# Graph attention in two layers: a closing product in seven half-size products, row maxima by way of DRAM, joins on VectorE, last residuals a unit ahead

## Chip, cores, metric

One core of a Trainium2 chip. The metric is the device time of one execution in microseconds (us), the median of several runs. "Before" took 1975.14 us (1974.1 to 1975.79) when the prediction was made.

## The reference

```python
def layer0(x, adj, weight):                    # N = 4096 rows, D = 512
    return relu(adj @ (max(sign(x), 0) @ sign(weight).T))
def layer1(x, adj, weight, bias, node_w, edge_w):
    node_att = softmax(x @ node_w, axis=0)
    h = x @ edge_w
    e = where(adj > 0, h @ h.T, NEG_BIG)
    return adj * (node_att * softmax(e, axis=1)) @ (x @ weight) + bias
x = layernorm(x + layer0(x, adj, ...))
x = layernorm(x + layer1(x, adj, ...))
```

Everything is float32. TensorE sets the time (it is busy for 1954.7 of 1974.9 us), so the kernel saves multiplications wherever it can: the large products use Strassen-like schemes with seven products for eight.

## The kernel before

It has four stretches. In the *first phase* (to about 500 us) layer 0 is summed up: `adj` is split in a rounded part `hi` and a rest `lo`, both stationary operands for the rows `xw`. Then come the scores `h @ h.T`, which go to DRAM (`s_d`) with their row maxima and sums. In the *main loop* (from 1079.6 us) four groups of four *blocks* reload scores, shift them by the row maximum, exponentiate, weigh by `adj` and multiply (tile `ps`). Each finished group is *joined* (seven additions) and gets its *closing product* with `w1`, whose instructions are put between those of the next group's blocks. The last group's closing product is the *tail*.

The row maxima `nm` stand one per partition. The shift needs them along the free dimension, the same line in all partitions. Before, TensorE did that:

```python
def panel(A):                                   # 512 rows: P = 128 partitions, BG = 4 row blocks
    nm = small.tile([P, BG], F32, name="nm")    # pool `small` has 2 buffers of each tile
    ...                                         # (cut: factor f of the softmax)
    spread = rows.tile([P, BG, P], F32, name="spread", tag="rows")
    nc.vector.tensor_copy(spread, nm.unsqueeze(2).to_broadcast([P, BG, P]))
    pt = ps_tr.tile([P, BG, P], F32, name="ptm", tag="tr")
    for i in range(BG):
        nc.tensor.transpose(pt[:, i, :], spread[:, i, :], ident)
    ...
    nc.scalar.copy(mrow.rearrange("p (b w) -> p b w", w=P), pt)

# the shift that uses the line, VectorE then ScalarE
    m = mrow.unsqueeze(1).to_broadcast([P, BG, W])
    pinned[0](nc.vector._custom_dve(TENSOR_ADD_SAT, out=q, in0=q, in1=m, s0=0.0, s1=-HUGE))
    nc.scalar.activation(q, q, AF.Exp)

# the closing product, one row block
    for k in range(KD):
        nc.tensor.matmul(po, (lower if k // 2 else upper)[:, k % 2, ts(i, P)], w1_s[:, k, :], ...)
    nc.vector.scalar_tensor_tensor(xb, po, f[:, i : i + 1], xb, ALU.mult, ALU.add)
```

## Time and profile before

| | before |
|---|---|
| time, median of 3 | 1975.14 us |
| TensorE busy | 1954.7 of 1974.9 us |
| first aggregation matmul starts at | 1079.6 us |
| main loop, first to last aggregation matmul | 854.3 us |
| tail | 41.0 us |

The last three are read from the start of the first and the end of the last `ps` matmul in the trace. Before the tail TensorE has no pause above 2.1 us. The page also has a picture of the span in 40 slices of 49 us; here are its rows for TensorE's busy tenths and the bytes moved by all DMA engines:

```profile
PE   9999999999999999999999999999999999999997
GB/s 312 297 322 304 305 320 315 296 327 279 154 266 201 189 284 255 225 258 287 198 365 310 351 270 236 269 253 196 217 264 253 212 252 236 225 288 206 160 60 64
```

### The profile page before, as it was taken

To read this page: it belongs to the slowest core of one execution; us is meant where nothing else is said; L and a number is where in the kernel's file an instruction comes from. 1 tells how busy PE (TensorE), PEld (TensorE's weight loads), DVE (VectorE), ACT (ScalarE), POOL (GpSimd) and SP (SyncE) were. 2 spreads that over 40 slices of the span, in tenths; PEclk is the share of its full clock that TensorE was granted. 3 is DMA by queue.
4 is the path that set the end of the run, shared out by engine and by line. 5 is a ranking of instruction groups with operands and counts; after the bars stand their busy time and mean duration, and the time that the engine had idled before them with its cause. 6 is when DMAs were issued, how large, how long until landed. Compare 5 with 4: busy or idle time off the path is not lost.

```text
span 1974.9 us, 18126 instructions
## 1 busy us (share of the span) xinstructions
PE 1954.7 (99%) x6122; PEld 1088.6 (55%) x6122; DVE 1365.8 (69%) x1992; ACT 672.7 (34%) x1107; POOL 402.4 (20%) x507
## 2 busy tenths in 40 slices
PE   9999999999999999999999999999999999999997
PEld 6888888888544455444555444444444444444443
DVE  7767667667764576667466986968678866967634
ACT  5433333333103576666677311121112211131100
POOL 0122222223341111101022111431124121411101
PEclk9999999999999999999999999999999999999999
DMA  8888888887475576677598976775677576675421
GB/s 312 297 322 304 305 320 315 296 327 279 154 266 201 189 284 255 225 258 287 198 365 310 351 270 236 269 253 196 217 264 253 212 252 236 225 288 206 160 60 64
DMA packets 133645, 497.71 MB, mean 252 GB/s; under 512 B 14000, under 2 KB 14000, under 8 KB 125872
## 3 DMA queue, kind: packets, MB, share of 16 engines
q0 software_dynamic: 71488, 262.17, 35.4%
q1 hardware_dynamic: 53712, 205.02, 31.0%
q10 hardware_dynamic: 8352, 29.36, 4.2%
q8 instruction: 48, 0.79, 0.2%
q14 instruction: 45, 0.37, 0.1%
HBM read 376.96 MB, written 119.54 MB: 251 GB/s over the span
## 4 chain that ended last, share of the span: by engine, by line
PE 91%; DMA 3%; issue 2%; DVE 2%; ACT 1%; POOL 1%; POOLq 0%; DVEq 0%; SPq 0%; ACTq 0%
PE ps L887 39%; PE seven L699 12%; PE acc L371 11%; PE acc L370 11%; PE po L940 5%; PE pe L630 4%; PE seven L98 4%; PE pt L600 2%; DMA s_d<-slot 2%; PE acc L243 1%; PE pw L211 1%; PE pt L330 1%; ACT line L571 1%; PE acc L244 1%; DMA more<-in_adj_dram 0%
## 5 line engine op out<-in xcount | busy, mean ns | idle before, releaser
L887 PE MATMUL ps<-lent,lop 128*128 128x512 f32 x960 | 419.3, 592 | 0.0
L370 PE MATMUL acc<-xw,hi 128*128 128x512 f32 x960 | 376.4, 392 | 0.0
L371 PE MATMUL acc<-xw,lo 128*128 128x512 f32 x960 | 374.3, 390 | 0.0
L887 PE MATMUL ps<-slot,lop 128*128 128x512 f32 x832 | 364.0, 592 | 0.0
L887 PEld LDWEIGHTS ps<-lent,lop 128*128 128x128 f32 x960 | 182.0, 190 | 227.2 <-issue 221.0
L887 PEld LDWEIGHTS ps<-slot,lop 128*128 128x128 f32 x832 | 157.8, 190 | 197.8 <-issue 193.2
L362 DVE TENSOR_TENSOR lo<-at,hi 128x1024 fp32r<-128x1024 f32 x120 | 147.0, 1225 | 84.4 <-ACT hi L360 84.3
L371 PEld LDWEIGHTS acc<-xw,lo 128*128 128x128 f32 x960 | 180.3, 188 | 37.1 <-DVE lo L362 0.3
L370 PEld LDWEIGHTS acc<-xw,hi 128*128 128x128 f32 x960 | 180.3, 188 | 36.8
L360 ACT CAST hi<-at 128x1024 fp32r<-128x1024 f32 x120 | 126.4, 1054 | 203.4 <-PE acc L370 148.4
L891 DVE TENSOR_TENSOR over<-over,ps 128x512 f32<-128x512 f32 x168 | 113.6, 680 | 94.0 <-PE ps L887 93.7
L804 ACT ACTIVATE lent<-lent 128x2048 f32<-128x2048 f32 x32 | 61.1, 1910 | 252.4 <-DVE lent L803 239.3
L630 PE MATMUL pe<-hT 128*128 128x512 f32 (+3 forms) x384 | 132.1, 486 | 0.0
L562 DVE CUSTOM_DVE_ANT_0 line<-lent,slot 128x512 f32<-128x512 bf16 x144 | 93.0, 688 | 45.9 <-ACT slot L640 23.0
L571 ACT ACTIVATE line<-line,nmax_c 128x512 f32<-128x512 f32 x160 | 114.8, 724 | 22.2 <-DVE nmax_c L562 22.1
L940 PE MATMUL po<-over 128*128 128x512 f32 x256 | 115.9, 600 | 3.2 <-DVE xb L949 3.2
L803 DVE CUSTOM_DVE_ANT_1 lent<-lent,line 128x2048 f32<-128x2048 f32 x32 | 80.9, 2527 | 49.6 <-DMA lent<-s_d 49.5
L804 ACT ACTIVATE slot<-slot 128x2048 f32<-128x2048 f32 x32 | 61.1, 1910 | 131.2 <-DVE slot L803 120.0
L699 PE MATMUL seven<-hT 128*128 128x512 f32 x192 | 89.8, 593 | 0.0
L630 PEld LDWEIGHTS pe<-hT 128*128 128x128 f32 x384 | 64.6, 191 | 41.4 <-issue 33.8
L940 PEld LDWEIGHTS po<-over 128*128 128x128 f32 x256 | 49.1, 192 | 65.9 <-issue 60.4
L803 DVE CUSTOM_DVE_ANT_1 slot<-slot,line 128x2048 f32<-128x2048 f32 x32 | 75.1, 2353 | 11.4 <-DMA slot<-s_d 10.2
(205 smaller groups left out, 2497.1 us busy)
## 6 DMA issues: line engine op xcount, KB each, us to landing
at<-in_adj_t_dram SPq DMA_DIRECT2D x60, 1024.0 KB, 7.2
lop<-lop_d SPq DMA_DIRECT2D x112, 512.0 KB, 3.9
lent<-in_adj_t_dram POOLq DMA_DIRECT2D x34, 1024.0 KB, 7.2
s_d<-slot POOLq DMA_DIRECT2D x33, 1024.0 KB, 7.0
slot<-s_d POOLq DMA_DIRECT2D x32, 1024.0 KB, 7.7
lent<-s_d POOLq DMA_DIRECT2D x32, 1024.0 KB, 8.3
slot<-in_adj_t_dram POOLq DMA_DIRECT2D x30, 1024.0 KB, 7.4
lent<-in_adj_dram SPq DMA_DIRECT2D x48, 512.0 KB, 5.0
```

The costliest lines, as they stand in the source:

```text
L360: nc.scalar.copy(hi, aq)
L362: nc.vector.tensor_sub(lo, aq, hi.bitcast(F32))
L370: nc.tensor.matmul(acc, hi[:, c, :], xw[:, kb, :], start=(kb == 0), stop=False)
L371: nc.tensor.matmul(acc, lo[:, c, :], xw[:, kb, :], start=False, stop=(kb == NB - 1))
L571: nc.scalar.activation(line, line, AF.Exp, bias=nmax_c[:, b, c : c + 1], scale=-1.0, accum_out=sum_c[:, b, c : c + 1])
L630: nc.tensor.matmul(pe[:, lo * P :], hT[:, k, ts(A * BG + i, P)], hT[:, k, (B * BG + lo) * P : (B + 1) * W], start=(k == 0), stop=(k == KD ...
L699: nc.tensor.matmul(ps, left[m][:, k, q, :], right[m][:, k, :], start=(first and k == 0), stop=(k == KD // 2 - 1), skip_group_check=not first,)
L803: pinned[0](nc.vector._custom_dve(TENSOR_ADD_SAT, out=q, in0=q, in1=m, s0=0.0, s1=-HUGE))
L804: nc.scalar.activation(q, q, AF.Exp)
L887: nc.tensor.matmul(ps, lop[:, c, ts(h, P)], rop[:, c, :], start=(c == 0), stop=(c == BG - 1))
L891: nc.vector.tensor_add(total[:, m, h, :], total[:, m, h, :], ps)
L940: nc.tensor.matmul(po, (lower if k // 2 else upper)[:, k % 2, ts(i, P)], w1_s[:, k, :], start=(k == 0), stop=(k == KD - 1),)
```

## The change

Four parts: eight quarter products of the closing product become seven of half width; the row maxima are written to DRAM and read back as a line into all partitions; the joins go from GpSimd to VectorE; the last group's residuals are loaded one block earlier. The steps put between the blocks also come twice as often, most of the normalizing moves to ScalarE, and the last outputs leave by SyncE's queue instead of GpSimd's. The core of the diff (the new class for the closing product is cut):

```diff
+    nm_d = [dram.tile([W], F32, name=f"nm_d{g}") for g in range(NG)]
@@ panel
-        spread = rows.tile([P, BG, P], F32, name="spread", tag="rows")
-        nc.vector.tensor_copy(spread, nm.unsqueeze(2).to_broadcast([P, BG, P]))
-        pt = ps_tr.tile([P, BG, P], F32, name="ptm", tag="tr")
-        for i in range(BG):
-            nc.tensor.transpose(pt[:, i, :], spread[:, i, :], ident)
         mrow = take(free_e)
-        nc.scalar.copy(mrow.rearrange("p (b w) -> p b w", w=P), pt)
+        nc.scalar.dma_start(nm_d[A].rearrange("(b p) -> p b", p=P), nm)
+        nc.gpsimd.dma_start(mrow, nm_d[A].unsqueeze(0).to_broadcast([P, W]))
@@ closing product (cut)
+            nc.vector.tensor_add(s1, l21, l22)          # and three more combinations
+            yield lambda: multiply("y", l11, 0, (a, 0))  # and six more half-width products
@@ normalizing, all but the last group
+                less = small.tile([P, n], F32, name="less")
+                nc.vector.scalar_tensor_tensor(less, mv[:, :, 0], -1.0, rstd, ALU.mult, ALU.mult)
+                nc.scalar.activation(xb, xb, AF.Identity, bias=less[:, k : k + 1], scale=rstd[:, k : k + 1])
@@ main loop
-            for queue, share in ((first, ...), (todo, count[0] % 2)):
+            for queue, share in ((first, ...), (todo, 1)):
-            todo.extend(lambda g=u.g, n=n: join(g, n, nc.gpsimd) for n in range(7))
+            todo.extend(lambda g=u.g, n=n: join(g, n, nc.vector) for n in range(7))
+        if n == len(blocks) - 2:
+            todo.extend(e.load for e in ends_)
```

More of the change, by code (lines that the diff above doesn't have):

```diff
@@ L772, in panel @@
         mrow = take(free_e)
-        nc.scalar.copy(mrow.rearrange("p (b w) -> p b w", w=P), pt)
+        nc.scalar.dma_start(nm_d[A].rearrange("(b p) -> p b", p=P), nm)
+        nc.gpsimd.dma_start(mrow, nm_d[A].unsqueeze(0).to_broadcast([P, W]))
         panels[A] = f, mrow
+        made[A] = now[0]
+    made = {}
     pinned = [tc.keep_in_program_order]
@@ L870, in landed, with known @@
                 return lambda: self.since[n] + 5 <= now[0]
+            def known(n):
+                return lambda: max(self.since[n], made[self.g + n % 2 * HG]) + 5 <= now[0]
             for k, n in enumerate(order):
-                yield landed(n), lambda n=n: self.shift(n)
+                yield known(n), lambda n=n: self.shift(n)
                 yield landed(4 + n), lambda k=k, n=n: self.weigh(n, order[k + 2] if k < 2 else None)
@@ L913, in join, with __init__ @@
         engine.tensor_tensor(out_, a, b, op)
+    spare = []
     class Finish:
-        def __init__(self, g, half, single=False):
-            self.g, self.half, self.A, self.single = g, half, g + half * HG, single
+        def __init__(self, g, half, last=False):
+            self.g, self.half, self.A, self.last = g, half, g + half * HG, last
+            self.stats = {}
         def steps(self):
             yield self.load
-            for i in range(BG):
-                yield lambda i=i: self.row(i)
-            if not self.single:
-                yield lambda: self.norm(range(BG))
+            for q in range(2):
+                yield from self.pair(q, ps_tr)
+            yield lambda: self.norm(range(BG))
         def load(self):
+            rows_ = x1_d[self.A * W : (self.A + 1) * W, :]
+            if self.last:
+                xb = take()
+                nc.gpsimd.dma_start(xb, rows_.rearrange("(b p) d -> p b d", p=P))
+                self.xbs = [xb[:, i, :] for i in range(BG)]
+                return
             self.xbs = []
@@ L931, in load @@
                 xb = rows.tile([P, D], F32, name="xb1", tag="rows")
-                nc.gpsimd.dma_start(xb, x1_d[ts(self.A * BG + i, P), :])
+                nc.gpsimd.dma_start(xb, rows_[ts(i, P), :])
                 self.xbs.append(xb)
-        def row(self, i):
-            t = sums[:, self.g % 2]
-            upper, lower = (t[:, 2], t[:, 4]) if self.half else (t[:, 1], t[:, 3])
-            po = ps_tr.tile([P, D], F32, name="po", tag="tr")
-            for k in range(KD):
-                nc.tensor.matmul(
-                    po,
-                    (lower if k // 2 else upper)[:, k % 2, ts(i, P)],
-                    w1_s[:, k, :],
-                    start=(k == 0),
-                    stop=(k == KD - 1),
-                )
-            f, _ = panels[self.A]
-            xb = self.xbs[i]
-            nc.vector.scalar_tensor_tensor(xb, po, f[:, i : i + 1], xb, ALU.mult, ALU.add)
-            if self.single:
-                self.norm([i])
@@ L953, in norm, with pair, combine, multiply @@
-        def norm(self, some_):
-            layernorm([self.xbs[i] for i in some_])
-            for i in some_:
-                nc.gpsimd.dma_start(out[ts(self.A * BG + i, P), :], self.xbs[i])
+        def pair(self, q, pool):
+            sums_g = sums[:, self.g % 2]
+            upper, lower = (sums_g[:, 2], sums_g[:, 4]) if self.half else (sums_g[:, 1], sums_g[:, 3])
+            a, b = q, q + 2
+            l11, l12, l21, l22 = (x[:, :, ts(i, P)] for i in (a, b) for x in (upper, lower))
+            tag = "tr" if pool is ps_tr else "mm"
+            bank, s = {}, []
+            def combine():
+                s.append(lopp.tile([P, 4, KD // 2, P], F32, name="left1", tag="lop"))
+                s1, s2, s3, s4 = (s[0][:, n] for n in range(4))
+                nc.vector.tensor_add(s1, l21, l22)
+                nc.vector.tensor_sub(s2, s1, l11)
+                nc.vector.tensor_sub(s3, l11, l21)
+                nc.vector.tensor_sub(s4, l12, s2)
+            def multiply(name, lop, rop, *to):
+                first = name not in bank
+                if first:
+                    x = name == "x"
+                    bank[name] = (ps_mm if x else pool).tile([P, HD], F32, name="po", tag="mm" if x else tag)
+                po = bank[name]
+                lop = lop if not isinstance(lop, int) else s[0][:, lop]
+                for k in range(KD // 2):
+                    nc.tensor.matmul(
+                        po,
+                        lop[:, k, :],
+                        w1_r[rop][:, k, :],
+                        start=(first and k == 0),
+                        stop=(k == KD // 2 - 1),
+                        skip_group_check=not first,
+                    )
+                f, _ = panels[self.A]
+                for i, h in to:
+                    xb = self.xbs[i][:, ts(h, HD)]
+                    nc.vector.scalar_tensor_tensor(xb, po, f[:, i : i + 1], xb, ALU.mult, ALU.add)
+            def half_stats(i, h):
+                if self.last:
+                    if i not in self.stats:
+                        if not spare:
+                            spare.append(take(free_e))
+                        at = 64 * (self.half * BG + i)
+                        self.stats[i] = spare[0][:, at : at + 12].rearrange("p (h s) -> p h s", h=2)
+                    nc.vector.bn_stats(self.stats[i][:, h, :], self.xbs[i][:, ts(h, HD)])
+                    if h == (0 if i == b else 1):
+                        self.norm([i])
+            yield combine
+            yield lambda: multiply("y", l11, 0, (a, 0))
+            yield lambda: (multiply("x", l12, 1, (a, 0)), half_stats(a, 0))
+            yield lambda: multiply("y", 1, 5, (a, 1))
+            yield lambda: multiply("z", 0, 4, (b, 1))
+            yield lambda: (multiply("y", 2, 6, (b, 1)), half_stats(b, 1))
+            yield lambda: (multiply("y", l22, 3, (b, 0)), half_stats(b, 0))
+            yield lambda: (multiply("z", 3, 2, (a, 1)), half_stats(a, 1))
@@ new lines, in norm @@
+        def norm(self, some_):
+            n = len(some_)
+            mv = small.tile([P, n, nc.vector.BN_AGGR_DIM], F32, name="mv")
+            for k, i in enumerate(some_):
+                if self.last:
+                    nc.vector.bn_aggr(mv[:, k, :], self.stats[i])
+                else:
+                    stats = small.tile([P, nc.vector.BN_STATS_DIM], F32, name="stats")
+                    nc.vector.bn_stats(stats, self.xbs[i])
+                    nc.vector.bn_aggr(mv[:, k, :], stats)
+            rstd = small.tile([P, n], F32, name="rstd")
+            nc.scalar.activation(rstd, mv[:, :, 1], AF.Sqrt, bias=eps)
+            nc.vector.reciprocal(rstd, rstd)
+            if not self.last:
+                less = small.tile([P, n], F32, name="less")
+                nc.vector.scalar_tensor_tensor(less, mv[:, :, 0], -1.0, rstd, ALU.mult, ALU.mult)
+            for k, i in enumerate(some_):
+                xb = self.xbs[i]
+                if self.last:
+                    nc.vector.tensor_scalar(xb, xb, mv[:, k, 0:1], rstd[:, k : k + 1], ALU.subtract, ALU.mult)
+                else:
+                    nc.scalar.activation(xb, xb, AF.Identity, bias=less[:, k : k + 1], scale=rstd[:, k : k + 1])
+                (nc.sync if self.last else nc.gpsimd).dma_start(out[ts(self.A * BG + i, P), :], xb)
@@ L1033 @@
     nc.sync.dma_start(w1_s, w1.rearrange("(k p) o -> p k o", p=P))
+    r11, r12, r21, r22 = (w1_s[:, k : k + 2, c : c + HD] for k in (0, 2) for c in (0, HD))
+    t2, t3, t4 = (take(free_e).rearrange("p (k o) -> p k o", o=HD) for _ in range(3))
+    w1_r = r11, r21, r22, t4, r12, t2, t3
+    todo.append(lambda: nc.vector.tensor_sub(t3, r22, r12))
+    todo.append(lambda: nc.vector.tensor_sub(r12, r12, r11))
+    todo.append(lambda: nc.vector.tensor_sub(t2, r22, r12))
+    todo.append(lambda: nc.vector.tensor_sub(t4, r21, t2))
+    ends_ = [Finish(HG - 1, half, True) for half in (1, 0)]
     for n, u in enumerate(blocks):
@@ L1051, in between @@
             count[0] += 1
-            for queue, share in ((first, -(-len(first) // (15 - count[0]))), (todo, count[0] % 2)):
+            for queue, share in ((first, -(-len(first) // (15 - count[0]))), (todo, 1)):
                 for _ in range(min(share, len(queue))):
@@ L1058 @@
         if u.r == HG - 1 and nxt:
-            todo.extend(lambda g=u.g, n=n: join(g, n, nc.gpsimd) for n in range(7))
+            todo.extend(lambda g=u.g, n=n: join(g, n, nc.vector) for n in range(7))
             for half in (1, 0):
                 todo.extend(Finish(u.g, half).steps())
-    for half in (1, 0):
-        todo.extend(Finish(HG - 1, half, half == 0).steps())
-    while todo:
-        todo.popleft()()
+        if n == len(blocks) - 2:
+            todo.extend(e.load for e in ends_)
+    assert not todo
+    for e in ends_:
+        for steps in zip(e.pair(0, ps_tr), e.pair(1, ps_mm)):
+            for step in steps:
+                step()
 def kernel(x, adj, L0_gnn_weight, L1_gnn_weight, L1_gnn_bias, L1_gnn_node_w, L1_gnn_edge_w):
```

## The prediction

> **What bounds the kernel now.** I read the page first (busy shares, then the chain of work that ended last), then the groups of instructions with shapes kept apart, then stretches of the timeline and a table of windows.
>
> ```profile
> span 1974.9 us, 18126 instructions
> PE 1954.7 (99%) x6122; PEld 1088.6 (55%) x6122; DVE 1365.8 (69%) x1992; ACT 672.7 (34%) x1107; POOL 402.4 (20%) x507
> ...
> PE 91%; DMA 3%; issue 2%; DVE 2%; ACT 1%; POOL 1%; POOLq 0%; DVEq 0%; SPq 0%; ACTq 0%
> ```
>
> TensorE has work for 1954.7 of 1974.9 us and 91% of the chain is its matmuls. So a microsecond is won only by giving TensorE fewer cycles, or in its 20 us of idle time, most of it at the two ends. The groups that the change touches:
>
> ```profile
> L887 PE MATMUL ps<-lent,lop 128*128 128x512 f32 x960 | 419.3, 592 | 0.0
> L940 PE MATMUL po<-over 128*128 128x512 f32 x256 | 115.9, 600 | 3.2 <-DVE xb L949 3.2
> L630 PE MATMUL pe<-hT 128*128 128x256 f32 x64 | 15.1, 379 | 0.0
> L769 PE MATMUL ptm<-ident,spread 128*128 128x128 f32 x32 | 4.9, 274 | 1.7 <-ACT slot L601 1.7
> L913 POOL TENSOR_TENSOR over<-over 128x1024 f32<-128x1024 f32 x21 | 67.4, 3218 | 10.9 <-DVE over L891 10.4
> L913 DVE TENSOR_TENSOR over<-over 128x1024 f32<-128x1024 f32 x7 | 8.6, 1224 | 0.2
> L949 DVE SCALAR_TENSOR_TENSOR xb<-po,f,xb 128x512 f32<-128x512 f32 x32 | 23.9, 747 | 16.6 <-PE po L940 9.9 <-DMA xb<-x_d 6.6
> ```
>
> The closing product is the second row. The order of instructions lists 128 matmuls for it and the trace 256, so each float32 matmul is recorded as two. Read spacing rather than duration: 600 ns is one matmul's latency, and they are pipelined. Row one gives 419.3/960 = 0.437 us each, tails included; from start to start in the timeline it is 0.429 us. For half the width there is a precedent in the diagonal blocks:
>
> ```profile
> 939.32 1.89 PE L630 MATMUL pe<-hT 128*128 128x256 f32 x8
> 941.04 0.49 PE L600 MATMUL pt<-ident,slot 128*128 128x128 f32 x3
> ```
>
> Eight records 256 wide take 941.04 - 939.32 = 1.72 us, 0.215 each: half width is half time, and the weight load (0.19 us) still hides.
>
> **What the Trainium skill says.** "TensorE: Matmul & The Clock Gate", section "Back-to-back issue gap", has the spacing set by weight load and matmul together, worse for narrow ones. Here, at 256 columns, the trace shows no penalty (0.215 against 0.429/2). "SBUF — State Buffer", section "SBUF: two separate sides", says that VectorE instructions with two SBUF inputs and GpSimd instructions that read SBUF lock each other out of a shared port pair for a whole instruction. The trace agrees:
>
> ```profile
> 1283.05 9.88 POOL L913 TENSOR_TENSOR over<-over 128x1024 f32<-128x1024 f32 x3 [2.82 <-DVE over L891]
> ...
> 1286.27 4.43 DVE L803 CUSTOM_DVE_ANT_1 slot<-slot,line 128x2048 f32<-128x2048 f32 x1
> ```
>
> ```profile
> 1316.31 2.28 DVE L803 CUSTOM_DVE_ANT_1 slot<-slot,line 128x2048 f32<-128x2048 f32 x1
> ```
>
> The same shift takes 4.43 us beside a join on GpSimd and 2.28 alone. I summed, over the VectorE instructions that overlap the 21 joins, what they take beyond the median of their form: 37.3 us, about 13 in each of the first two groups. "DMA: Bandwidth & Descriptors", sections "Anatomy of one DMA — SWDGE (gpsimd) path" and "Rules for kernel authors", gives about 2.0 us fixed cost for a DMA and one descriptor for each element of a non-contiguous write. The row maxima now make such a write (512 elements of 4 bytes) and a read after it. No transfer of this trace is that small: the smallest listed, 128 KB, take 5.9 and 6.5 us to land.
>
> **The change part by part.**
>
> *Closing product.* Eight quarter products become seven: for each of the 8 panels, 2 pairs of row blocks times 7 products times 2 matmuls, 224 matmuls of 256 columns, 448 records at 0.215 = 96.3 us, against 256 at 0.429 = 109.8. That saves 13.5 us, an eighth, not a half. Three quarters of it (10.1 us) lie in the main loop, where TensorE never idles and so each cycle counts. The last quarter is in the tail, judged apart.
>
> *Row maxima.* The 32 transposes go: 32 x 0.109 spacing = 3.5 us, and the 1.7 us wait before one of them. In their place VectorE's first shift of a group waits for a write and a read through DRAM. The first shift stands two steps of 3.4 us behind the panel. If it waits 2 to 4 us more, TensorE does not notice: six PSUM banks of 3.4 us each lie between. Together -5.2 us.
>
> *VectorE.* Joins: 7 x 1.22 = +8.5 us a group, and the 13 us of lock-out go. Combinations of the left factor: 16 of 128x256 at about 0.41 (these widths take 418 to 487 ns in this trace, some overlapped) = +6.5. Additions to the residual: 28 half width, estimated at 747 minus 256/0.96 = 480 ns, about 0.42 as they overlap, 11.8, against 8 x 0.67 = 5.4: +6.4. Normalizing moves to ScalarE: 8 x 0.48 = -3.9. Spread copy -0.8. Sum +3.7 us a group. Today's load:
>
> ```profile
> 1272.80:1320.90 48.10, 48.10 (x114) 21.30 (x113) 38.81 (x27) 12.93 (x15) 21.61 (x14) 1.00 0.65 224
> 1320.90:1382.70 61.80, 61.80 (x146) 27.36 (x145) 46.08 (x61) 10.80 (x10) 8.87 (x14) 1.00 0.66 234
> 1382.70:1444.50 61.80, 61.80 (x146) 27.36 (x145) 37.63 (x57) 8.32 (x8) 10.34 (x16) 1.00 0.68 236
> 1444.50:1493.40 48.90, 48.90 (x121) 22.04 (x120) 45.49 (x43) 12.42 (x8) 15.99 (x12) 1.00 0.75 259
> ```
>
> These are the four blocks of the second group; the columns are window, length, then TensorE, weight loads, VectorE, ScalarE, GpSimd. VectorE is busy 168 of 220.6 us and would be about 172 of 216: 80%, not a bound on average. GpSimd's queue, which also starts the big loads, loses 9 us and more of joins that stood ahead of those loads.
>
> *Tail.* Call T the end of the last aggregation matmul (1933.9). Now:
>
> ```profile
> 1956.91 0.75 DVE L949 SCALAR_TENSOR_TENSOR xb<-po,f,xb 128x512 f32<-128x512 f32 x1 [5.01 <-DMA xb<-x_d]
> 1957.72 0.30 PEld L940 LDWEIGHTS po<-over 128*128 128x128 f32 x2 [4.01 <-DVE xb L949]
> 1957.72 8.83 PE L940 MATMUL po<-over 128*128 128x512 f32 x16 [3.19 <-DVE xb L949]
> ```
>
> The last residuals arrive late, TensorE idles 3.2 us and then runs 16 matmuls in 8.83 us instead of about 7. The last scaling ends at 1969.4 (T+35.5) and the output lands at T+41. The early load removes this wait. But VectorE now has, after T: the last addition and join (2.0 us), 28 half-width additions (11.8), 7 left combinations (2.9), 16 half-width statistics (6.5), 8 aggregations (1.6), 8 reciprocals (1.4), 8 scalings (4.0), together 30 us, more than TensorE's 112 x 0.215 = 24. With a few waits for each other: last scaling at T+31 to T+34, end 5.5 us later, T+36.5 to T+39.5. The tail, now VectorE's, gives about -2.5 us, not the 5 that the removed stall promises.
>
> **A new wait.** The seven products of a pair add into two banks, one of them in use four times. TensorE can't go on with that bank until VectorE has read it, with one or two steps (4.3 us each) between. Today each row has its own bank and plenty of time: in the timeline, VectorE's pass over a closed row starts up to 8.2 us after the row's last matmul, mostly 4 to 8. The order of VectorE's instructions in the changed kernel puts the first read of the bank behind a shift whose load starts when TensorE frees a buffer. By rows of the page: issue 0.75 + landing 8.3 + shift 2.3 + read 0.45 = 11.8 us, while TensorE reaches the product that needs it 3 x 3.44 + 2 x 0.86 = 12.0 us after the release. That is a tie. I put stalls at 5 us over three groups (0 to 12).
>
> **Sum.** 1975.1 - 10.1 - 5.2 - 2.5 + 5 = 1962.3; I say 1963.
>
> **Rivals.**
> First, the bank wait dominates. VectorE's lag of 4 to 8 us today speaks for it: made good by TensorE waiting in each group, it would cost 12 to 24 us, for 1968 to 1982. Against it: part of the lag comes from the lock-out and from loads that stood behind joins (before the shift at 1316.31 VectorE also waited 4.94 us for a mask whose load was issued right after three joins), and both go.
> Second, VectorE, relieved of the lock-out, keeps up everywhere and nothing stalls: 1957. For it: 80% load. Against it: blocks one and four of a group already have VectorE at 81% and 93%, in bursts.
> Third, the row maxima arrive late, so the shift and all behind it slip: some 3 us a group at worst, since TensorE has 17 us of banks. Up to 1972.
> Fourth, half-width matmuls cost more than half when two of them stand between full ones: at 0.25 us each, 448 would take 112 us and the gain of the product would be gone, for about 1973. The eight consecutive ones at 0.215 speak against it.
>
> **Range and chances.** The gain in TensorE cycles is sure within a microsecond or two; stalls (0 to 12) and tail (-5 to +3) set the range: 1953 to 1975. For 2% faster it would have to lose 39 us, more than everything touched could give; 2% slower needs stalls of over 55 us. Faster 0.02, same 0.96, slower 0.02.
>
> **What would show it.** Closing product: 448 records and near 100 us busy. Transposes of row maxima gone. In the main loop, waits of TensorE or its weight loads on the closing product's reads by VectorE: none to 4 us a group; above 5 a group the first rival is right. VectorE shifts: no 4.4 us ones left. Tail: from the last aggregation matmul to the end 36.5 to 39.5 us, VectorE nearly always busy, TensorE waiting for it. I am wrong if the closing product takes over 105 us, if aggregation matmuls wait for their operands, or if the tail grows beyond 41 us.

## More of the kernel before

The program is written in an order which a scheduler then changes: an instruction can move ahead as far as its data and buffers allow.

Slices 20 to 23 (from 938 to 1135 us: 198, 365, 310, 351) are the passage from scores to main loop. There scores are stored and the first blocks loaded at once.

## The result, and the profile after

The changed kernel took 2038.05 us (median of 4, 2033.3 to 2042.31) against 1975.47 us for the kernel before in the same rounds: ratio 1.0314, 95% interval 1.0286 to 1.0342. It is slower by 3%, and far outside the predicted range. (A ratio is the mean time of one kernel's runs over that of the other's of the same rounds, so it isn't quite the ratio of the medians.)

The page of the changed kernel: span, busy times and chain.

```profile
span 2033.4 us, 18671 instructions
...
PE 1957.6 (96%) x6282; PEld 1124.0 (55%) x6282; DVE 1383.4 (68%) x2146; ACT 687.9 (34%) x1126; POOL 330.9 (16%) x480
...
PE 77%; DMA 10%; issue 6%; DVE 5%; ACT 2%; POOL 1%; POOLq 0%; SPq 0%; DVEq 0%; ACTq 0%
```

TensorE has no more work than before (1957.6 against 1954.7 us), yet the span grew by 58.5 us. In the chain DMA rose from 3 to 10%. The slices show where:

```profile
PE   9999999999999999999967499999999999999998
...
PEclk9999999999999999999988799999999999999999
...
GB/s 309 295 306 304 298 314 296 299 318 253 173 238 217 199 310 195 269 264 314 112 343 210 214 274 282 234 248 235 230 213 280 222 246 203 290 248 206 237 93 42
```

TensorE pauses in slices 21 to 23 only, and in slices 20, 22 and 23 DMA moves 112, 210 and 214 GB/s where it moved 198, 310 and 351. (The clock row falls where TensorE pauses. By the trace the clock follows the pause here: in the first long one it is halved from 3.8 us after the last matmul until 5.8 us after the next one starts, and 512-wide matmuls then start every 0.853 us instead of 0.429.) TensorE's timeline around two of its pauses in the changed kernel, the idle time in square brackets:

```profile
1032.69 5.32 PE L631 MATMUL pe<-hT 128*128 128x512 f32 x12
1053.10 1.12 PE L601 MATMUL pt<-ident,lent 128*128 128x128 f32 x4 [15.09 <-ACT lent L641]
```

```profile
1139.43 4.03 PE L890 MATMUL ps<-lent,lop 128*128 128x512 f32 x9
1169.87 2.90 PE L890 MATMUL ps<-slot,lop 128*128 128x512 f32 x3 [26.41 <-ACT lent L804]
```

ScalarE is only the messenger. The chain of waits of the changed kernel, in order of time (start, length, what), shows what it waited for:

```profile
1009.68 1.73 PE seven L700 x4
1011.43 25.76 DMA lop<-lop_d
1037.19 5.72 DMA s_d<-lent
...
1052.64 13.07 DMA s_d<-slot
...
1067.58 21.35 DMA line<-nm_d
...
1115.22 13.08 DMA s_d<-slot
...
1131.43 27.34 DMA s_d<-lent
```

Five of these six loads and stores take 13 to 27 us, where the same kinds land in 4.4 us (`lop<-lop_d`) or 6.6 us (`s_d<-slot` of 1 MB) by the median of their rows. The windows view compares the stretch from 1002 to 1022 us, before and after (the last number is GB/s, the one ahead of it the share of the DMA engines' time):

```profile
1002.00:1022.00 20.00, 20.00 (x82) 11.77 (x81) 14.35 (x37) 15.54 (x38) 4.16 (x6) 1.00 1.02 402
```

```profile
1002.00:1022.00 20.00, 17.81 (x60) 8.64 (x59) 9.90 (x30) 11.91 (x30) 2.53 (x4) 1.00 0.80 27
```

The DMA engines count as busy for 80% of the time and move 27 GB/s instead of 402. In the packets of the trace, 4 KB take 0.16 us before by the median; in this stretch of the changed kernel the median is 1.0 us, and 46 of its 131 packets of 4 KB take 2 to 6.3 us. GpSimd's queue, which carries the scores, starts none at all. The 537 packets of 4 bytes there add up to 4 of 255 us: the profile books the time on their neighbours. What ran just before are the new writes of the row maxima. The instructions by tile, and the list of DMA issues with KB and median us to landing:

```profile
L769 ACTq DMA_DIRECT2D nm_d<-nm x8: 366/372/1014, 1000.6 to 1142.9; - x8
...
DMA to landing us min/median/max: 3.6/11.2/23.9
```

```profile
nm_d<-nm ACTq DMA_DIRECT2D x8, 2.0 KB, 15.2
```

All eight writes run between 1000.6 and 1142.9 us. The code asks for six of them later, one pair a group, but they depend on nothing but `nm`, and the scheduler moved them ahead, into the busiest stretch of transfers. (The transposes of the kernel before stand one pair of panels a group, from 1036.6, 1227.3, 1447.9 and 1668.5 us.)

From the two traces, piece by piece (starts of matmuls; a wait is the time between two starts beyond the usual spacing):

| piece | before | after | difference |
|---|---|---|---|
| the 1920 `acc` matmuls of the first phase, busy | 750.7 | 761.0 | +10.3 |
| all else before the first `ps` matmul (1079.6, 1122.6) | 328.9 | 361.6 | +32.7 |
| waits in the first block of the main loop | 0 | 29.2 | +29.2 |
| rest of the main loop | 854.3 | 851.0 | -3.3 |
| tail | 41.0 | 30.6 | -10.4 |
| span | 1974.9 | 2033.4 | +58.5 |

"Rest of the main loop" holds the predicted parts: six closing products of 12.0 instead of 13.7 us (-10.3), three groups of transposes gone (0.8 each, -2.4), and waits of TensorE in the blocks with closing products (+9.4).

The first row of the table is another surprise. The same instructions with the same operands take longer, in a phase that the change does not touch. Page of before, then of after (busy us, mean ns of one):

```profile
L370 PE MATMUL acc<-xw,hi 128*128 128x512 f32 x960 | 376.4, 392 | 0.0
L371 PE MATMUL acc<-xw,lo 128*128 128x512 f32 x960 | 374.3, 390 | 0.0
```

```profile
L372 PE MATMUL acc<-xw,lo 128*128 128x512 f32 x960 | 380.5, 396 | 0.0
L371 PE MATMUL acc<-xw,hi 128*128 128x512 f32 x960 | 380.5, 396 | 0.0
```

### The profile page after: what moved, and what is told of

Read it like the earlier page. It is cut to its first block, busy times and chain, and to the rows that moved or that the text cites.

```text
span 2033.4 us, 18671 instructions
## 1 busy us (share of the span) xinstructions
PE 1957.6 (96%) x6282; PEld 1124.0 (55%) x6282; DVE 1383.4 (68%) x2146; ACT 687.9 (34%) x1126; POOL 330.9 (16%) x480
## 4 chain that ended last, share of the span: by engine, by line
PE 77%; DMA 10%; issue 6%; DVE 5%; ACT 2%; POOL 1%; POOLq 0%; SPq 0%; DVEq 0%; ACTq 0%
PE ps L890 28%; PE seven L700 12%; PE acc L372 11%; PE acc L371 11%; PE seven L99 5%; PE po L972 3%; PE pe L631 2%; PE pt L601 2%; DMA s_d<-slot 2%; DMA s_d<-lent 2%; DMA lent<-in_adj_t_dram 2%; DMA lop<-lop_d 1%; DMA slot<-in_adj_t_dram 1%; DMA line<-nm_d 1%; PE acc L244 1%
## 5 line engine op out<-in xcount | busy, mean ns | idle before, releaser
L890 PE MATMUL ps<-slot,lop 128*128 128x512 f32 x832 | 368.1, 596 | 26.4 <-ACT lent L804 26.4
L372 PE MATMUL acc<-xw,lo 128*128 128x512 f32 x960 | 380.5, 396 | 0.0
L371 PE MATMUL acc<-xw,hi 128*128 128x512 f32 x960 | 380.5, 396 | 0.0
L894 DVE TENSOR_TENSOR over<-over,ps 128x512 f32<-128x512 f32 x168 | 113.9, 679 | 59.9 <-PE ps L890 59.7
L631 PE MATMUL pe<-hT 128*128 128x512 f32 (+3 forms) x384 | 137.0, 501 | 0.0
L803 DVE CUSTOM_DVE_ANT_1 lent<-lent,line 128x2048 f32<-128x2048 f32 x32 | 73.2, 2287 | 43.0 <-DMA lent<-s_d 43.0
L601 PEld LDWEIGHTS pt<-ident,lent 128*128 128x128 f32 x412 | 51.5, 142 | 83.7 <-issue 37.8
L601 PE MATMUL pt<-ident,lent 128*128 128x128 f32 x412 | 62.9, 276 | 30.8 <-ACT lent L641 28.2
L803 DVE CUSTOM_DVE_ANT_1 slot<-slot,line 128x2048 f32<-128x2048 f32 x32 | 73.1, 2286 | 27.6 <-DMA slot<-s_d 25.6
```

The costliest lines, as they stand in the source:

```text
L371: nc.tensor.matmul(acc, hi[:, c, :], xw[:, kb, :], start=(kb == 0), stop=False)
L372: nc.tensor.matmul(acc, lo[:, c, :], xw[:, kb, :], start=False, stop=(kb == NB - 1))
L601: nc.tensor.transpose(pt[:, j, :], src[:, ts(j, P)], ident)
L631: nc.tensor.matmul(pe[:, lo * P :], hT[:, k, ts(A * BG + i, P)], hT[:, k, (B * BG + lo) * P : (B + 1) * W], start=(k == 0), stop=(k == KD ...
L890: nc.tensor.matmul(ps, lop[:, c, ts(h, P)], rop[:, c, :], start=(c == 0), stop=(c == BG - 1))
L894: nc.vector.tensor_add(total[:, m, h, :], total[:, m, h, :], ps)
```

## The experiments

**Theory**: the 512 pieces of 4 bytes of a write of row maxima hold up all DMA queues for some 10 to 20 us, and TensorE waits for the other transfers. Separately, something makes the first phase 10 us slower. **Rivals**: the round trip itself (a shift that waits for its line, or VectorE waiting in order for one of two buffers of `nm`); or the other parts of the change (joins, closing product).

| run | base | time (us) | before (us) | ratio, 95% interval |
|---|---|---|---|---|
| e1_turns | after | 1983.35, 5 runs | 1976.36 | 1.0037 (1.0024 to 1.0050) |
| e2_dram | before | 2027.44, 4 runs | 1976.36 | 1.0265 (1.0248 to 1.0282) |
| e3_pad | before | 1986.33, 4 runs | 1976.36 | 1.0052 (1.0037 to 1.0067) |
| e4_lines | after | 1985.24, 4 runs | 1976.36 | 1.0039 (1.0024 to 1.0054) |
| e5_write | before | 2006.43, single look | 1976.73 | |
| e6_write16 | before | 1977.16, single look | 1976.73 | |
| e7_nm8 | after | 2034.51, single look | 1976.73 | |
| e8_signs | before | 1987.72, single look | 1976.73 | |
| e9_turns_low | after | 1971.00, 12 runs | 1976.32 | 0.9975 (0.9965 to 0.9985) |
| e10_lines_low | after | 1975.52, 13 runs | 1976.32 | 0.9996 (0.9988 to 1.0004) |
| e12_joins | after | 2012.38, 4 runs | 1976.32 | 1.0183 (1.0170 to 1.0196) |
| e13_mixed | after | 1965.32, 6 runs | 1976.32 | 0.9949 (0.9936 to 0.9961) |
| e14_apart | before | 1979.84, single look | 1980.41 | |
| e15_512x16 | before | 1983.99, single look | 1980.41 | |

All give the correct result.

### Which part of the change? e1_turns and e2_dram

The changed kernel with the old row maxima:

```diff
-        nc.scalar.dma_start(nm_d[A].rearrange("(b p) -> p b", p=P), nm)
-        nc.gpsimd.dma_start(mrow, nm_d[A].unsqueeze(0).to_broadcast([P, W]))
+        # spread, four transposes, copy: as in the kernel before
```

> The changed kernel with the row maxima turned on TensorE as before, everything else of the change kept. If the 4-byte writes of the row maxima are what stops the DMA engines and through them TensorE, the 33 us of waits before the main loop and the 29 us in its first block go: 2038 - 62 plus up to 5 us of transposes, 1975 to 1982 us, and 10 us of that is the slower first phase, which should stay (L372-like rows at 0.233 us a record). If joins on VectorE, the closing product or the earlier loads were to blame, it stays above 2020 us.

The kernel before with the new row maxima alone (the same diff the other way):

> The kernel before with only the row maxima by DRAM, nothing else changed. The write theory: 1975 + 62 - up to 5 us = 2030 to 2040 us, with the first block of the main loop near 77 us long instead of 48; first phase at 0.227 us a record as before. If other parts of the change are to blame: 1970 to 1980 us.

Measured: 1983.35 and 2027.44 us. Taking the round trip out of the changed kernel gives back 55 us; putting it alone into the kernel before costs 51. In e2_dram TensorE pauses 18.0 and 14.5 us before the main loop, and waits 15.8 in its first two blocks. (The first block is 59.7 us long, not near 77 as I expected: the pauses fall elsewhere. e1_turns is 1 us above its expected range, e2_dram 3 us below.) So the row maxima are the cause; joins and closing product are not, and that rival falls.

### The write, or what waits for it? e4_lines, e7_nm8, e5_write

e4_lines keeps the round trip but writes four pieces of 512 bytes:

```diff
-        nc.scalar.dma_start(nm_d[A].rearrange("(b p) -> p b", p=P), nm)
+        turned = ps_tr.tile([P, P], F32, name="ptm", tag="tr")
+        nc.tensor.transpose(turned[:BG, :], nm, ident)
+        line = rows.tile([P, BG, P], F32, name="spread", tag="rows")[:BG, 0, :]
+        nc.scalar.copy(line, turned[:BG, :])
+        nc.scalar.dma_start(nm_d[A].rearrange("(b p) -> b p", p=P), line)
```

> The changed kernel, but the row maxima are turned to four lines of 128 on TensorE (one 128x4 transpose a panel) and written as four descriptors of 512 bytes; the round trip by DRAM, the broadcast read and the waits for them stay. The write theory: the stops of the DMA engines go, 1970 to 1978 us (10 us of it the first phase). The rival, that the round trip itself or the in-order wait for it costs the time: above 2020 us.

Measured: 1985.24 us, 53 below the changed kernel but 7 above the top of what I expected. TensorE still waits 6.1 us in the first block. This run alone doesn't settle it: its `line` tile comes from the pool of `spread`, so the scheduler no longer moves the writes ahead, and two things changed at once.

e7_nm8 leaves the write and its place alone and gives `nm` eight buffers:

```diff
-        nm = small.tile([P, BG], F32, name="nm")
+        nm = pan.tile([P, BG], F32, name="nm", bufs=NG)
```

> The changed kernel with eight buffers for the row maxima instead of two, in another pool, so VectorE never waits for a write to land before it makes the next panel's. Through that move the later tiles also lie where they lay before, which should give back the 10 us of the first phase. The write theory: the stops stay, 2038 - 10 = 2022 to 2032 us. The rival, VectorE held up by the two buffers: below 2005 us.

Measured: 2034.51 us in a single look, 2.5 above the expected range, with pauses of TensorE of 21.7, 22.5 and 25.3 us. The first phase is back at its old speed, which should have given 10 us; the pauses took most of that. VectorE did wait for a buffer of `nm` in the changed kernel (16.5 us, once, in the waits by tile), but this wait isn't what costs the time.

e5_write adds the same write to the kernel before, whose transposes stay. Nobody reads what it writes:

```diff
+    nm_d = [dram.tile([W], F32, name=f"nm_d{g}") for g in range(NG)]
@@ panel, at its end
+        nc.scalar.dma_start(nm_d[A].rearrange("(b p) -> p b", p=P), nm)
         panels[A] = f, mrow
```

> The kernel before, with its transposes of the row maxima, plus the writes of the changed kernel (512 of 4 bytes a panel) whose result nobody reads or waits for. If the writes alone stop the DMA engines: 2020 to 2040 us, with several waits of TensorE of 8 us and more around the start of the main loop. If the cost is the round trip (the read, and what waits for it): 1976 us.

Measured: 2006.43 us in a single look, 30 above before; TensorE pauses 12.9 and 12.0 us ahead of the main loop. The write alone does it. It is less than the 51 of e2_dram, and the first expectation (2020 to 2040) was too high: without the read, no shift waits for a line, the first block of the main loop has no wait at all. And two of its eight writes run only at 1461 us: they took 14.3 and 13.2 us to land, but TensorE lost nothing there (the main loop is as long as before's, within 0.1 us). So what such a write costs depends on when it runs. One of the two pauses of e5_write goes through the rival's door: in its chain of waits the next panel's `nm` waits 18.1 us for the write to land. So both effects have one root, a write of 2 KB that takes 14 us to land and holds up nearly all else.

### What about the write? e6_write16, e14_apart, e15_512x16

The three vary e5_write: 128 pieces of 16 bytes; 512 pieces of 4 bytes, but 512 bytes apart in DRAM; 512 pieces of 16 bytes side by side.

```diff
-        nc.scalar.dma_start(nm_d[A].rearrange("(b p) -> p b", p=P), nm)
+        nc.scalar.dma_start(nm_d[A].rearrange("(p b) -> p b", b=BG), nm)                          # e6_write16
+        nc.scalar.dma_start(nm_d[A][:, 0:1].rearrange("(b p) o -> p b o", p=P), nm.unsqueeze(2))  # e14_apart, nm_d is [W, 128]
+        nc.scalar.dma_start(nm_d[A].rearrange("(b p) f -> p b f", p=P), nm4)                      # e15_512x16, nm4 holds each value four times
```

> As e5_write, but the same 2 KB are written in the order of the partitions: 128 pieces of 16 bytes. If each piece costs alike, the stops are a quarter as long, 2 to 3 us, which the loads' lead should hide: 1976 to 1982 us. If the bytes or the single write cost, it is as slow as e5_write.

> As e5_write (512 pieces of 4 bytes a panel, nobody reads them), but each piece is written 512 bytes from the next in DRAM instead of beside it. If neighbouring pieces disturb one another (several writes into one line of memory), the stops go: 1976 to 1980 us. If the number or the size of the pieces counts: as slow as e5_write, 2000 to 2012 us.

> As e5_write, but each of the 512 pieces has 16 bytes (the value four times), 8 KB side by side in DRAM. If the number of the pieces counts, 2000 to 2012 us as e5_write; if it is their size of 4 bytes, 1976 to 1980 us, as e6_write16 with its 128 pieces.

Measured: 1977.16, 1979.84 and 1983.99 us, where before had 1976.73 and 1980.41. (e15_512x16 fits neither branch of its expectation.) Here are 10 us after the first pair of writes (they begin 0.7 to 2.5 us after the second write), for e5_write, e6_write16, e14_apart and e15_512x16 in this order; the last number is GB/s:

```profile
994.00:1004.00 10.00, 10.00 (x39) 5.42 (x38) 7.96 (x25) 9.20 (x24) 2.43 (x4) 1.00 0.94 74
```

```profile
994.00:1004.00 10.00, 9.99 (x36) 4.98 (x35) 7.10 (x21) 9.99 (x25) 2.71 (x5) 1.00 1.01 359
```

```profile
992.50:1002.50 10.00, 10.00 (x39) 5.42 (x38) 8.05 (x26) 9.07 (x22) 3.31 (x5) 1.00 0.99 330
```

```profile
993.50:1003.50 10.00, 10.00 (x39) 5.28 (x37) 7.53 (x25) 9.70 (x25) 2.83 (x5) 1.00 1.02 310
```

Only e5_write falls to 74 GB/s. And the issues of the row maxima in e5_write and e14_apart (the last number is the median us to landing):

```profile
nm_d<-nm ACTq DMA_DIRECT2D x8, 2.0 KB, 14.3
```

```profile
nm_d<-nm ACTq DMA_DIRECT2D x8, 2.0 KB, 5.8
```

Neither the number of pieces (e14_apart has as many) nor their size of 4 bytes (e14_apart has the same) is enough: it takes 4-byte pieces that lie side by side in DRAM (whether far fewer of them would do, no run shows). With 16 bytes a piece, side by side, at most a few us are left. TensorE has one pause that neither before nor e6_write16 has, 3.1 us in e14_apart and 3.8 in e15_512x16. In their chains of waits it goes back to the rival's door: the next `nm` (or `nm4`) waits 9.3 and 11.9 us until the write before has landed and its buffer is free. That is a wait for two buffers, not a stop of transfers. The Trainium skill, "DMA: Bandwidth & Descriptors", section "Specifications", says that SDMA does a read-modify-write below 512 bytes. That alone would have e14_apart as slow as e5_write, which the run contradicts. That many such writes to the same few lines of memory queue up behind one another would fit, but no run shows the inside of the memory, so it stays a guess.

### The first phase: e3_pad and e8_signs

The changed kernel has one tile more in the pool `small` (`less`, 16 bytes in two buffers, 64 bytes with rounding), so by the compiled programs' addresses every later tile lies 64 bytes higher. e3_pad does only that to the kernel before, e8_signs moves only the pool of `hi` and `lo`:

```diff
+    nc.vector.memset(small.tile([P, BG], F32, name="less"), 0.0)     # e3_pad, at the start
+        nc.vector.memset(sp.tile([P, BG], F32, name="pad"), 0.0)     # e8_signs, first tile of the pool of hi and lo
```

> The kernel before with one unused 64-byte tile pair in the small pool (set to zero once), so that all later tiles of SBUF lie 64 bytes higher, as they do in the changed kernel. If the placement makes the 10 us of the first phase: 1984 to 1987 us, and the 0.227 us a record become 0.233. If not (something of the run or the clock): 1975 us.

> The kernel before with 64 unused bytes ahead of the pool that holds hi and lo alone, the stationary operands of the first phase's products; nothing else moves. If the address of these two tiles makes the 0.235 us a record of e3_pad: 1985 to 1988 us. If another shifted tile does it, 1976 us and 0.228 us a record.

Measured: 1986.33 and 1987.72 us (the second a single look). The two groups in e8_signs:

```profile
L372 PE MATMUL acc<-xw,lo 128*128 128x512 f32 x960 | 380.9, 397 | 0.0
L371 PE MATMUL acc<-xw,hi 128*128 128x512 f32 x960 | 380.8, 397 | 0.0
```

That is the slow row of the changed kernel (380.5 and 380.5), from 64 bytes of address alone (the moving operand `xw` stays at the same address in all kernels). `hi` starts at bytes 217,664 and 221,760 of a partition in the fast kernels, 64 more in the slow ones, and `lo` 8,192 bytes below; in the fast ones the address leaves a rest of 64 when divided by 128, in the slow ones no rest. Only these two placements were run, so this is no rule yet, and why it matters is open. It is not one bad run: all five kernels with the high address (the changed one, e1, e3, e4, e8) have 396 or 397 ns in both groups, the eleven others 392 and 390.

### What is the rest of the change worth? e9_turns_low, e10_lines_low, e13_mixed, e12_joins

e9_turns_low and e10_lines_low are e1_turns and e4_lines without the new tile:

```diff
-                less = small.tile([P, n], F32, name="less")
+                less = mv[:, :, 1]
```

> e1_turns with its added small tile put into a column that already exists, so that hi and lo lie where they lay before: both losses are out, and what is left is the rest of the change. 1983.4 - 10.4 = 1973 us (1970 to 1976), so the other three parts together are worth some 3 us only: 10 us from the closing product and 10 us from the tail, less 10 to 17 us of new waits for PSUM banks. If the placement had other effects, 1978 us or more.

> e4_lines with the same move of the small tile: 1985.2 - 10.4 = 1975 us (1970 to 1977), and 0.227 us a record in the first phase.

Measured: 1971.00 us (0.25% faster than before) and 1975.52 us (the same). The placement is worth 12 and 10 us here, as expected. That e10_lines_low is slower than e9_turns_low although it spares TensorE 24 transposes has a reason that its page shows in what VectorE's shift waited for:

```profile
L807 DVE CUSTOM_DVE_ANT_1 slot<-slot,line 128x2048 f32<-128x2048 f32 x32 | 73.1, 2286 | 29.8 <-DMA line<-nm_d 17.0 <-DMA slot<-s_d 12.7
```

17.0 us go to the line from DRAM. TensorE loses most in the first group: the main loop starts at 1086.7 us against 1078.6 in e9_turns_low, and its first block has 8.2 us of waits against 4.9. There, I argued, the maxima are known just before they are needed, in the stretch where the queues are full. So e13_mixed turns the first group's two panels on TensorE and sends the other six by DRAM in four lines each:

```diff
+        if A % HG == 0:
+            # spread, four transposes, copy: as in the kernel before
+        else:
+            # one transpose, a write of four lines, the read: as in e4_lines
```

> e10_lines_low with the maxima of the first group of panels turned on TensorE as before, since that group's round trip by DRAM is the one that nothing hides (6 us of wait in the first block of e4_lines, 2 us in e1_turns). 4 to 6 us faster than e10_lines_low: 1968 to 1972 us, faster than the kernel before by 0.2 to 0.4 per cent.

Measured: 1965.32 us, 0.51% faster than before (ratio 0.9949), 10 us faster than e10_lines_low, twice what I expected. It beats both kernels. Its page:

```profile
span 1963.5 us, 18692 instructions
...
PE 1940.0 (99%) x6296; PEld 1122.0 (57%) x6296; DVE 1383.7 (70%) x2148; ACT 691.3 (35%) x1134; POOL 331.2 (17%) x478
```

TensorE has 14.7 us less work than before (1954.7) and 3.3 us more idle time. The main loop starts at 1078.4 us; TensorE waits 5.5 us in its first block and 6.3 in those with closing products.

e12_joins is e10_lines_low with the joins back on GpSimd:

```diff
-            todo.extend(lambda g=u.g, n=n: join(g, n, nc.vector) for n in range(7))
+            todo.extend(lambda g=u.g, n=n: join(g, n, nc.gpsimd) for n in range(7))
```

> e10_lines_low with the joins back on GpSimd. If the joins on VectorE are what makes the products of the closing product wait for their banks, these waits (4.7 us in e4_lines outside its first block) shrink and it is 2 to 4 us faster than e10_lines_low. If VectorE's lock-out by GpSimd was the larger cost, as the prediction has it (13 us of VectorE a group against 9 us for the seven joins), it is as fast or up to 6 us slower.

Measured: 2012.38 us, 37 slower than e10_lines_low, against an expectation of up to 6. The first block of each of the three groups is 11.7 to 13.1 us longer by waits of TensorE. GpSimd's joins and, by what they wait for, the matmuls of the closing product in e12_joins:

```profile
L920 POOL TENSOR_TENSOR over<-over 128x1024 f32<-128x1024 f32 x21 | 70.9, 3389 | 18.4 <-DVE over L898 17.8
```

```profile
L976 PE MATMUL po<-line,left 128*128 128x256 f32 x128 | 35.4, 407 | 21.2 <-DVE xb L987 21.2
...
L976 PE MATMUL po<-line,over 128*128 128x256 f32 x64 | 16.9, 389 | 4.8 <-DVE xb L987 4.8
```

The seven joins of a group take 24 us on GpSimd and 9 on VectorE, and the changed kernel starts the closing product after seven steps of 3.4 us, twice as soon as the kernel before. TensorE then waits 26.0 us (21.2 and 4.8) for VectorE to read a product's bank. What puts VectorE behind? The trace speaks for the lock-out of the prediction: VectorE's instructions that overlap the joins take 13.9, 14.0 and 12.3 us a group beyond the median of their form. Two of its instructions beside a join in e12_joins, and two of the same kind in e10_lines_low:

```profile
1295.16 5.01 DVE L814 SCALAR_TENSOR_TENSOR lent<-slot,lent 128x512 f32<-128x512 f32 x2
```

```profile
1294.68 1.28 DVE L814 SCALAR_TENSOR_TENSOR lent<-slot,lent 128x512 f32<-128x512 f32 x2
```

No run separates this from the late joins, and the scheduler also ordered VectorE's instructions differently. What is shown: with the new closing product started this soon, the joins cost 37 us on GpSimd. In this order of steps the move to VectorE isn't a small gain but a condition of the rest.

## Why the prediction was wrong, point by point

*The step that failed* is the one on the row maxima: "In their place VectorE's first shift of a group waits for a write and a read through DRAM ... If it waits 2 to 4 us more, TensorE does not notice ... Together -5.2 us." It measured the new write by its consumer's wait alone. The runs showed +51 us for this part alone (e2_dram), for a reason on which no step of the prediction bears: 512 neighbouring pieces of 4 bytes a write hold up nearly all other transfers (27 against 402 GB/s). One of the signs by which the prediction said it would be wrong came true: aggregation matmuls waited for their operands, 29.2 us in the first block. The prediction had noted one descriptor for each element, and that no transfer of the trace was that small; that was the place to widen the range instead of taking the landing time of a 128 KB transfer for a guide. It also took the writes to run one pair a group, where "TensorE has 17 us of banks", while the scheduler put all eight into the fullest stretch of transfers. The order of instructions of the changed kernel, which can be seen before a run, would have shown this. The third rival ("some 3 us a group at worst", up to 1972 us) has the right part and less than a fifth of the size (9 us against 51). The chance of 0.02 for slower stood on "2% slower needs stalls of over 55 us", and 61.9 us were lost about the start of the main loop (32.7 before it, 29.2 in its first block; the first includes the matmuls at half clock).

*A term that was missing*: +10.3 us in the first phase, from a 16-byte tile that moved `hi` and `lo` by 64 bytes (e3_pad, e8_signs). Nothing in the profile of before could tell it, but the addresses in the compiled program did shift.

*Closing product*: -10.1 us in the loop predicted; 10.3 measured (six products of 12.0 against 13.7 us). Right. The four rows of its matmuls add up to 448 records of 256 columns, as said, and the fourth rival (half-width matmuls that cost more than half) is out. But the sign "I am wrong if the closing product takes over 105 us" was badly chosen: the rows' busy times add up to 113.6 us, since each burst of four counts to the end of its last matmul (1.03 us) while the next matmul starts 0.86 us after its beginning. By the prediction's own advice, read the spacing.

*New wait*: 5 us (0 to 12) predicted; 9.4 us in the changed kernel, 4.7 in e4_lines, 6.3 in e13_mixed. Right in kind and about in size; none of these has the 12 to 24 us of the first rival. The waits stand where the prediction put them, here in the changed kernel:

```profile
L972 PE MATMUL po<-line,left 128*128 128x256 f32 x128 | 32.4, 381 | 1.9 <-DVE xb L983 1.9
...
L972 PE MATMUL po<-line,over 128*128 128x256 f32 x64 | 16.9, 389 | 5.1 <-DVE xb L983 5.1
```

*VectorE*: "no 4.4 us ones left" holds; the longest of the 64 shifts takes 2.29 us. The half-width additions last 0.476 us and overlap, near the 0.42 that the prediction counted. The group of shifts of which some were at 4.4 us, before and after (mean ns of one):

```profile
L803 DVE CUSTOM_DVE_ANT_1 lent<-lent,line 128x2048 f32<-128x2048 f32 x32 | 80.9, 2527 | 49.6 <-DMA lent<-s_d 49.5
```

```profile
L803 DVE CUSTOM_DVE_ANT_1 lent<-lent,line 128x2048 f32<-128x2048 f32 x32 | 73.2, 2287 | 43.0 <-DMA lent<-s_d 43.0
```

*Tail*: -2.5 us predicted (T+36.5 to T+39.5); it measured T+30.6, so -10.4. The mechanism was right (the early load removes the wait, VectorE sets the end: it is busy 26.6 of the 30.6 us), the sizes weren't. VectorE's instructions overlap a little more than I counted (26.6 against 30 us), its last scaling ends at T+27.6 instead of T+31 to 34, and the last output lands 3.0 us after that, not 5.5 (it now leaves by SyncE's queue):

```profile
2027.61 3.12 SPq L1027 DMA_DIRECT2D out_dram<-lent  x4
...
2029.82 0.55 DVE L1024 TENSOR_SCALAR lent<-lent,mv,rstd 128x512 f32<-128x512 f32 x1
```

*The sum*: with the two losses taken out, and the row maxima of three groups still by DRAM, the change is worth what was predicted: e13_mixed has 1965.32 us, the prediction 1963. The terms for the closing product and the new wait were good to a few us each; a tail that was 8 us better than said made up for 5.5 us of wait in the first block and for the transposes that stay. So it is in part luck that the sum fits.

## What to carry to other kernels

Before sending a small result through DRAM, look at its pieces: one value of 4 bytes a partition, written side by side, can hold up nearly every other transfer for 10 to 20 us. The same values 16 bytes at a time (e6_write16, one look), or turned into four lines of 512 bytes, held up nothing that shows, though in e10_lines_low VectorE still waited 17.0 us for the lines to come back. A transfer must be judged by what it does to its neighbours and by when the scheduler will really issue it, not by its consumer's slack alone. When an untouched phase gets slower, compare the addresses of its operands first: a new small tile shifts everything allocated after it.

## What the Trainium skill lacked or had wrong

- "DMA: Bandwidth & Descriptors": it has the one descriptor per element and the read-modify-write below 512 bytes, but not that 4-byte writes side by side in DRAM hold up the transfers of all queues (74 GB/s in e5_write, 27 in the changed kernel, where the median of 4 KB packets went from 0.16 to 1.0 us), nor that the same pieces 512 bytes apart don't (330 GB/s in e14_apart). That stalled writes hold up an engine's other queues it says of remote DMA alone (section "Back-pressure in remote DMA").
- No page that I read has an effect of a stationary float32r operand's address on the time of its matmuls: 64 bytes more, 396 instead of 390 and 392 ns a record, 10.3 us over 1920 records (e3_pad, e8_signs). "SBUF — State Buffer", section "Operand start alignment", treats the address as a matter of legality and says that its runs timed nothing.
